# Attention with a conditioning token: another order of the score products in the last bursts of one core

## The chip, the cores and the metric

One NeuronCore of a Trainium2 chip runs the whole kernel; the other cores are idle. The metric is the device time of one execution in microseconds (us), as the median of several runs. All arithmetic but two small helpers is float32.

## The reference

`x` has shape (8, 512, 512): 8 batches, 512 rows, 512 features, which are 16 heads of 32. One token per batch, `cond_1024`, is projected and added to every row's query and key.

```python
Q = split_heads(x @ Wq.T + bq);  K = split_heads(x @ Wk.T + bk);  V = split_heads(x @ Wv.T + bv)
cQ = Q + split_heads(tokens @ Wq.T + bq)
cK = K + split_heads(tokens @ Wk.T + bk)
scores = einsum('bhqd,bhkd->bhqk', cQ, cK) / sqrt(32)
out = einsum('bhqk,bhkd->bhqd', softmax(scores, axis=-1), V)
return x + merge_heads(out)
```

## The kernel before

**Tiles.** The work is cut into T = 32 tiles `t`: 8 batches times 4 groups of 4 heads. The 4 heads of a tile lie in the 4 strips of 32 partitions, so a product over one head's 32 features uses one strip of 32 rows of TensorE's array, and the products of four heads can be in the array side by side. `qkT["q", t]` and `qkT["k", t]` hold a tile's transposed queries and keys.

**The softmax of one tile** goes in two passes over its scores. First the row maxima: `row_max(t, qc)` multiplies the queries of row block `qc` (128 rows, 4 blocks a tile) with all 512 keys, one product for each head (L499, in `row_scores`), each into a bank of PSUM, and VectorE (DVE) reduces the banks to negated maxima `nmax`: as two pairs of banks (L508, `row_max_of`), or for most tiles and the very last row block as two single banks (L490) and one pair. When the 4 blocks of a tile are done, `split_max` cuts the maxima into three bfloat16 parts (L532 to L535, on GpSimd (POOL), for the last tile on DVE), and `transpose_max` turns them with TensorE (L544) and copies them out as `maxT` (L550). Then the exponentials: `exponentials(t, kc)` computes the transposed scores of key block `kc`, for each head a product of `onesb` and `maxT` that writes the negated maxima into the bank (L560, bfloat16) and the score product added on top (L563), and ScalarE (ACT) takes the exponentials out of the four banks (L574, four instructions) into `e` tiles. `times_v(t, kc, ...)` multiplies them with V (L579); the 4 heads there use 4 strips of 32 columns.

A float32 product of 512 columns is two matmul instructions in the trace, a first and a second pass, each with its own weight load, so four heads show as x8.

**The order** is written out by hand. Each engine runs its instructions in program order (`tc.manual_schedule`), with the waits that the framework derives from tiles and PSUM banks. The main loop runs over t = 0 to 28. In a step a burst `exponentials(t, kc)`, `row_max(...)` is followed by projection products or by products with V. `TURNS` says which of the 8 banks a step uses: entries 0 to 3 are the banks of the four heads' scores in `exponentials`, entries 4 to 7 those of `row_max`; `banks(i, n)` reads the current row, and `row(i)` sets it to row 8 + i. The products after the burst use a bank of entries 0 to 3 whose exponentials are out.

**The last three tiles** (t = 29, 30, 31) have no projections left and stand below the loop. `part_of(t, bank, kcs)` multiplies some key blocks with V, ACT copies the bank out (L775, or L769 and an addition on POOL, L770); `masked` (L600, POOL), `spread_sums` (L610) and `denominators_of` (L780) make the denominators of tile 28 and 29, and `send_parts` divides (L785, L635 on DVE, L636 and L637 on POOL) and stores. For tiles 30 and 31 the denominators are sums of `e` tiles (`sum_of`, L845 and L847, mostly on DVE; L845 once on POOL) times a matrix of ones (`times_ones`, L589).

The bursts there, in order, with the tile and key block of the exponentials and the tile and row block of the maxima:

| burst | exponentials | maxima | after it |
|---|---|---|---|
| A | 29, 0 | 30, 1 | two products with V |
| B | 29, 1 | 30, 2 | one product with V |
| C | 29, 2 | 30, 3 | `split_max(30)` on POOL, one product with V, `spread_sums` |
| D | 29, 3 | 31, 0 | one product with V, `transpose_max(30)`, one more |
| E | 30, 0 | 31, 1 | two products with V, `spread_sums` |
| F | 30, 1 | 31, 2 | one product with V |
| G | 30, 2 | 31, 3 | `split_max(31)` on DVE, one product with V |
| H | 30, 3 | none | one product with V, then `transpose_max(31)` |
| I to L | 31, 0 to 3 | none | products with V and with ones |

Of the kernel before, what the change touches and what calls it, by code (L numbers as in the profile page):

```python
# [9 lines left out]
F32 = mybir.dt.float32  # L10
BF16 = mybir.dt.bfloat16
AF = mybir.ActivationFunctionType
ALU = mybir.AluOpType
AX = mybir.AxisListType
# [3 lines left out]
def kernel(  # L18
# [38 lines left out]
    nc = tc.nc  # L57
    P = 128
    B, S, D = x.shape
    HD = 32  # L60
    H = D // HD
    G = D // P
    HG = P // HD
# [12 lines left out]
    ep = ctx.enter_context(tc.tile_pool(name="ep", bufs=13))  # L76
# [15 lines left out]

# [4 lines left out]

# [11 lines left out]
    turn = [0]  # L109

    def banks(i, n=1):

        j = TURNS[turn[0]][i]
        if n == 1:
            return psum[:, j, :]
        k = TURNS[turn[0]][i + 1]
        return psum[:, j : k + 1 : k - j, :]
# [83 lines left out]
    onesb = const.tile([P, P], BF16, tag="onesb", name="onesb")  # L201
# [43 lines left out]
    for i in range(NS):  # L245
        r = slice(i * BL, (i + 1) * BL)
# [92 lines left out]
    qkT = {}  # L339
# [134 lines left out]
    nmax = {}  # L474
    sums = {}

    def open_max(t):
        if t not in nmax:
            nmax[t] = op.tile([P, NS, HG, 1], F32, tag="nmax", name=f"nmax_{t}", bufs=3)
            sums[t] = op.tile([P, NS, HG, 1], F32, tag="sums", name=f"sums_{t}", bufs=3)  # L480

    def row_max(t, qc):
        if t >= T:
            return
        open_max(t)
        for j in range(HG):
            row_scores(t, qc, j, banks(HG + j))
        if t < T - 2 or t * NS + qc == T * NS - 1:
            for j in range(2):
                nc.vector.tensor_reduce(  # L490
                    nmax[t][:, qc, j : j + 1, 0], banks(HG + j), AX.X, ALU.max, negate=True
                )
        else:
            row_max_of(t, qc, 0, banks(HG, 2))
        row_max_of(t, qc, 1, banks(HG + 2, 2))

    def row_scores(t, qc, j, pt):
        r = slice(j * HD, (j + 1) * HD)
        nc.tensor.matmul(  # L499
            pt,  # L500
            qkT["q", t][r, qc * P : (qc + 1) * P],
            qkT["k", t][r, :],
            start=True,
            stop=True,
        )

    def row_max_of(t, qc, pr, pt):
        nc.vector.tensor_reduce(  # L508
            nmax[t][:, qc, pr * 2 : pr * 2 + 2, 0], pt, AX.X, ALU.max, negate=True
        )  # L510
# [26 lines left out]
    maxT = {}  # L537

    def transpose_max(t, bank, copy=nc.vector.tensor_copy):
        if t >= T:  # L540
            return
        pt = bank.bitcast(BF16)
        for qc in range(NS):
            nc.tensor.transpose(  # L544
                pt[:, qc * P : (qc + 1) * P],
                split[t % 2][:, qc, :, :].rearrange("p h e -> p (h e)"),
                identb,
            )
        maxT[t] = op.tile([P, S], BF16, tag="maxT", name=f"maxT_{t}")
        copy(maxT[t], pt[:, :S])  # L550


    es = {}

    def exponentials(t, kc, at=None):

        bank = [psum[:, i, :] for i in at] if at else [banks(i) for i in range(HG)]
        for j in range(HG):
            r = slice(j * HD, j * HD + 3)
            nc.tensor.matmul(bank[j], onesb[r, :], maxT[t][r, :], start=True, stop=False)  # L560
        for j in range(HG):
            r = slice(j * HD, (j + 1) * HD)
            nc.tensor.matmul(  # L563
                bank[j],
                qkT["k", t][r, kc * P : (kc + 1) * P],
                qkT["q", t][r, :],
                start=False,
                stop=True,
            )
        for pr in range(NP):  # L570
            e = ep.tile([P, 2, S], F32, tag="e", name=f"e_{t}_{kc}_{pr}")
            es[t, kc, pr] = e
            for i in range(2):
                nc.scalar.activation(e[:, i, :], bank[pr * 2 + i], AF.Exp)  # L574

    def times_v(t, kc, pt, chunks=range(NS)):
        b, g = divmod(t, G)
        for j in range(HG):
            nc.tensor.matmul(  # L579
                pt[j * HD : (j + 1) * HD, :],  # L580
                vs[b % 2][:, kc, (g * HG + j) * HD : (g * HG + j + 1) * HD],
                es[t, kc, j // 2][:, j % 2, :],
                start=(kc == chunks[0]),
                stop=(kc == chunks[-1]),
            )
# [11 lines left out]
    def masked(t):  # L597

        apart = op.tile([P, HG, NS, NS], F32, tag="apart", name=f"apart_{t}")
        nc.gpsimd.tensor_tensor(  # L600
            apart,
            sums[t].rearrange("p c h o -> p h c o").broadcast_to([P, HG, NS, NS]),
            which.unsqueeze(1).unsqueeze(1).broadcast_to([P, HG, NS, NS]),
            ALU.mult,
        )
        return apart

    def spread_sums(apart, pd):
        for h in range(HG):
            nc.tensor.matmul(  # L610
                pd[h * BL : (h + 1) * BL, :NB],
                modulo,
                apart[:, h].rearrange("p c a -> p (c a)"),
                start=True,
                stop=True,
            )
# [63 lines left out]
    def bank(i):  # L680
        return psum[:, i, :]
# [48 lines left out]
        pass  # L730


    turn[0] = 12
    row_max(0, 0)
    turn_w("v", [1, 2, 3])
    combine_w("v")
# [24 lines left out]
    def part_of(t, pt, of, between=None):  # L761

        for k, kc in enumerate(of):
            if k and between:
                between()
            times_v(t, kc, pt, of)
        if t in parts:
            p = op.tile([P, S], F32, tag="dead", name=f"part_{t}_{of[0]}")
            nc.scalar.copy(p, pt)  # L769
            nc.gpsimd.tensor_tensor(parts[t], parts[t], p, ALU.add)  # L770
        else:
            if not parts:
                parts["all"] = stage.tile([P, NC, D], F32, tag="w", name="parts")
            parts[t] = parts["all"][:, t % NC, :]
            nc.scalar.copy(parts[t], pt)  # L775
# [12 lines left out]
    for t in range(T - 3):  # L788
        b, r = divmod(t, G)
# [52 lines left out]
    def sum_of(t, to, kc, on, prs=range(NP)):  # L842
        for pr in prs:
            if kc == 1:
                on.tensor_tensor(to[pr], es[t, 0, pr], es[t, 1, pr], ALU.add)  # L845
            else:
                on.tensor_tensor(to[pr], to[pr], es[t, kc, pr], ALU.add)  # L847
# [5 lines left out]
    def row(i):  # L853
        turn[0] = 8 + i

    t = T - 3
    row(0)
    exponentials(t, 0)
    row_max(t + 1, 1)
    part_of(t - 1, banks(0), [0, 1])  # L860
    load_residual(t + 1)
    load_residual(t + 2)
    row(1)
    exponentials(t, 1)
    row_max(t + 1, 2)
    part_of(t - 1, banks(0), [2])
    apart = masked(t - 1)
    row(2)
    exponentials(t, 2)
    row_max(t + 1, 3)  # L870
    split_max(t + 1)
    part_of(t - 1, banks(0), [3])
    spread_sums(apart, banks(1))
    den = denominators_of(t - 1, banks(1))
    row(3)
    exponentials(t, 3)
    row_max(t + 2, 0)
    part_of(t, banks(0), [0, 1], lambda: transpose_max(t + 1, banks(1), nc.scalar.copy))
    send_parts(t - 1, den)

    t = T - 2
    row(0)
    exponentials(t, 0)
    row_max(t + 1, 1)
    apart = masked(t - 1)
    part_of(t - 1, banks(0), [2, 3])
    spread_sums(apart, banks(1))
    den = denominators_of(t - 1, banks(1))
    row(1)
    exponentials(t, 1)  # L890
    row_max(t + 1, 2)
    acc = room_for_sums(t)
    sum_of(t, acc, 1, nc.gpsimd, [0])
    part_of(t, banks(0), [0])
    send_parts(t - 1, den)
    row(2)
    exponentials(t, 2)
    row_max(t + 1, 3)
    split_max(t + 1, nc.vector)
    pa, rest = banks(0), [1, 2, 3]  # L900
    times_v(t, 1, pa, rest)

    exponentials(t, 3, (1, 2, 3, 4))
    times_v(t, 2, pa, rest)
    transpose_max(t + 1, bank(5), nc.vector.tensor_copy)
    sum_of(t, acc, 1, nc.vector, [1])
    sum_of(t, acc, 2, nc.vector)

    t = T - 1
    exponentials(t, 0, (6, 7, 1, 2))  # L910
    times_v(t - 1, 3, pa, rest)
    nc.vector.tensor_tensor(parts[t - 1], pa, parts[t - 1], ALU.add)
    sum_of(t - 1, acc, 3, nc.vector)
    exponentials(t, 1, (3, 4, 5, 6))
    pv = bank(7)
    times_v(t, 0, pv)
    acc2 = room_for_sums(t)
    sum_of(t, acc2, 1, nc.vector)
    exponentials(t, 2, (1, 2, 3, 0))
    times_v(t, 1, pv)  # L920
    pd = bank(5)
    times_ones(acc, pd, True, True)
# [18 lines left out]
            queue.dma_start(spread(out[b], g * P + h * BL), y30[h * BL : (h + 1) * BL])  # L941

    store_30(nc.sync, (0, 1))
    exponentials(t, 3, (4, 6, 1, 2))
    times_v(t, 2, pv)
    pd = bank(3)
    times_ones(acc2, pd, True, False)
    times_ones([es[t, 3, pr] for pr in range(NP)], pd, False, True)
    times_v(t, 3, pv)
# [5 lines left out]
    nc.vector.tensor_copy(oT[:, two[0]], pv[:, two[0]])  # L955
    nc.scalar.copy(oT[:, two[1]], pv[:, two[1]])
    store_30(nc.scalar, (2, 3))
    pi, po = bank(0), [bank(4), bank(6)]
    untranspose(den, pi)
    rec = op.tile([P, NS, HG, 1], F32, tag="rec", name="rec")  # L960
    nc.vector.reciprocal(
# [52 lines left out]
```

## Time and profile before

| what | value |
|---|---|
| time, median of 3 runs | 731.7 us (731.52 to 732.57) |
| time of the profiled execution | 731.48 us |
| its span, first to last instruction | 729.7 us |
| mean granted TensorE clock | 0.999 |

The tail, by stretches of the span, busy us of each engine (PE is TensorE's matmuls, PEld its weight loads):

| stretch | PE | DVE | ACT | POOL |
|---|---|---|---|---|
| 680.5 to 706.5, bursts A to G | 26.00 | 17.35 | 18.42 | 12.24 |
| 706.5 to 723.5, bursts H to L | 16.20 | 16.25 | 10.98 | 2.17 |
| 723.5 to 729.7, last output | 1.44 | 2.16 | 0.37 | 1.44 |

How to read it: "busy" of PE runs from a matmul's start to a modelled end, so small idle times between bursts hardly show in it; they show as the bracket behind a row of the timeline, which gives the idle time just before it and what released it. In a row `PE L499 MATMUL psum<-kT,qT 32*128 32x512 f32 x8`, L499 is the line, `psum` what is written, `kT,qT` what is read, and x8 the number of instructions that follow each other.

### The profile page before, as it was taken

What the parts mean: (1) busy time and instruction counts of PE and PEld (TensorE: products, weight loads), DVE (VectorE), ACT (ScalarE), POOL (GpSimd) and SP (SyncE); (2) the same over time, 40 slices, a digit from 0 to 9 for tenths busy, and PEclk for the clock granted to TensorE, in tenths of its full rate; (3) what the DMA queues carried; (4) which work ended last, traced back from release to release, by engine and by line L of the source; (5) the groups of instructions that cost most, each with busy time, mean ns of one, the idle gap of its engine ahead of it and who ended that gap; (6) DMA issues with size and microseconds to landing.
All of it is one profiled execution on the core that took longest, in us unless ns stands there. A gap on an engine that the chain in (4) does not pass through costs nothing.

```text
span 729.7 us, 15089 instructions
## 1 busy us (share of the span) xinstructions
PE 722.4 (99%) x5396; PEld 402.0 (55%) x5396; DVE 536.9 (74%) x859; ACT 617.3 (85%) x1540; POOL 176.4 (24%) x276
## 2 busy tenths in 40 slices
PE   9999999999999999999999999999999999999997
PEld 5566555566555566555566555566555566555432
DVE  4798777777778777688676777677777777667677
ACT  2589898899898898898899898898898899898664
POOL 3711221122221122221122221122221122221351
PEclk9999999999999999999999999999999999999999
DMA  7733221222221222221222221222110111110121
GB/s 183 121 56 65 45 44 23 37 41 34 45 41 26 38 37 37 45 44 23 37 41 34 44 42 26 37 37 37 30 30 8 24 30 30 30 24 14 23 30 30
DMA packets 208111, 29.64 MB, mean 41 GB/s; under 512 B 205722, under 2 KB 206746, under 8 KB 208036
## 3 DMA queue, kind: packets, MB, share of 16 engines
q1 hardware_dynamic: 206400, 27.88, 23.9%
q10 hardware_dynamic: 1636, 0.81, 0.4%
q8 instruction: 42, 0.69, 0.4%
q14 instruction: 33, 0.27, 0.1%
HBM read 20.27 MB, written 8.39 MB: 39 GB/s over the span
## 4 chain that ended last, share of the span: by engine, by line
PE 97%; DVE 2%; issue 1%; DMA 1%; DVEq 0%
PE psum L406 26%; PE psum L499 16%; PE psum L579 15%; PE psum L563 15%; PE psum L403 14%; PE psum L560 6%; PE psum L350 2%; PE psum L544 1%; DVE acc L847 1%; DMA x<-in_x_dram 1%; PE psum L266 0%; DVE acc L845 0%; PE psum L311 0%; PE psum L657 0%; PE psum L589 0%
## 5 line engine op out<-in xcount | busy, mean ns | idle before, releaser
L518 ACT ACTIVATE dead<-psum,nmax 128x512 f32<-128x512 f32 x480 | 327.0, 701 | 5.4 <-DVE nmax L490 3.0
L574 ACT ACTIVATE e<-psum 128x512 f32<-128x512 f32 x512 | 264.3, 603 | 75.7 <-PE psum L563 75.6
L490 DVE TENSOR_REDUCE nmax<-psum 128x1 f32<-128x512 f32 x242 | 155.9, 686 | 143.2 <-PE psum L499 143.2
L508 DVE TENSOR_REDUCE nmax<-psum 128x2 f32<-128x1024 f32 x135 | 163.5, 1216 | 9.5 <-PE psum L499 8.2
L636 POOL TENSOR_TENSOR res<-res,recs 128x512 f32<-128x512 f32 x30 | 31.4, 1047 | 439.9 <-DVE res L635 439.9
L499 PE MATMUL psum<-kT,qT 32*128 32x512 f32 x1024 | 136.3, 601 | 0.0
L563 PE MATMUL psum<-qT,kT 32*128 32x512 f32 x1024 | 132.4, 588 | 0.0
L579 PE MATMUL psum<-e,v 128*32 128x512 f32 x1024 | 121.2, 596 | 0.0
L518 ACT ACTIVATION_READ_ACCUMULATOR dead<-psum,nmax 128x1 f32 x480 | 104.9, 218 | 0.0
L499 PEld LDWEIGHTS psum<-kT,qT 32*128 32x128 f32 x1024 | 58.1, 183 | 56.2 <-ACT dead L518 19.9
L579 PEld LDWEIGHTS psum<-e,v 128*32 128x32 f32 x1024 | 26.7, 110 | 65.8 <-issue 38.4
L563 PEld LDWEIGHTS psum<-qT,kT 32*128 32x128 f32 x1024 | 51.0, 185 | 2.2
L560 PE MATMUL psum<-maxT,onesb 3*128 3x512 bf16 x512 | 51.7, 384 | 0.5 <-DVE maxT L550 0.5
L403 PE MATMUL psum<-wc_v,xc 128*128 128x256 f32 x192 | 49.3, 379 | 0.0
L560 PEld LDWEIGHTS <-onesb 3*128 3x128 bf16 x512 | 13.4, 90 | 61.1 <-issue 51.7
L406 PE MATMUL psum<-xc,wc_k 128*128 128x256 f32 x180 | 46.2, 379 | 0.0
L406 PE MATMUL psum<-xc,wc_q 128*128 128x256 f32 x180 | 46.2, 379 | 0.0
L174 POOL TENSOR_TENSOR xr<-xr,bvs 128x512 f32<-128x512 f32 x31 | 39.3, 1268 | 17.8 <-DMA xr<-in_x_dram 17.8
L403 PEld LDWEIGHTS psum<-wc_v,xc 128*128 128x128 f32 x192 | 36.5, 190 | 5.0
L637 POOL TENSOR_TENSOR res<-res,xr 128x512 f32<-128x512 f32 x30 | 38.3, 1275 | 2.4
L403 PE MATMUL psum<-wT_v,xT 128*128 128x256 f32 x128 | 38.8, 405 | 0.0
L406 PEld LDWEIGHTS psum<-xc,wc_k 128*128 128x128 f32 x180 | 34.2, 190 | 4.6
(163 smaller groups left out, 775.2 us busy)
## 6 DMA issues: line engine op xcount, KB each, us to landing
xr<-in_x_dram SPq DMA_DIRECT2D x124, 64.0 KB, 2.4
out_dram<-res SPq DMA_DIRECT2D x122, 64.0 KB, 2.0
x<-in_x_dram SPq DMA_DIRECT2D x112, 64.0 KB, 2.5
w_q<-in_L_cond_Wq_dram SPq DMA_DIRECT2D x4, 256.0 KB, 4.5
w_v<-in_L_cond_Wv_dram SPq DMA_DIRECT2D x16, 64.0 KB, 2.4
w_k<-in_L_cond_Wk_dram SPq DMA_DIRECT2D x16, 48.0 KB, 2.2
x<-in_x_dram ACTq DMA_DIRECT2D x2, 256.0 KB, 4.3
x<-in_x_dram SPq DMA_DIRECT2D x2, 256.0 KB
```

Source lines behind the costliest of these rows:

```text
L174: nc.gpsimd.tensor_tensor(xr[t], xr[t], bias, ALU.add)
L403: nc.tensor.matmul(pt, xb, w, start=(kc == kcs[0]), stop=(kc == kcs[-1]))
L406: nc.tensor.matmul(pt, w, xb, start=(kc == kcs[0]), stop=(kc == kcs[-1]))
L490: nc.vector.tensor_reduce(nmax[t][:, qc, j : j + 1, 0], banks(HG + j), AX.X, ALU.max, negate=True)
L499: nc.tensor.matmul(pt, qkT["q", t][r, qc * P : (qc + 1) * P], qkT["k", t][r, :], start=True, stop=True,)
L508: nc.vector.tensor_reduce(nmax[t][:, qc, pr * 2 : pr * 2 + 2, 0], pt, AX.X, ALU.max, negate=True)
L518: nc.scalar.activation(dead, banks(HG + j), AF.Exp, bias=nmax[t][:, qc, j, :], accum_out=sums[t][:, qc, j, :],)
L560: nc.tensor.matmul(bank[j], onesb[r, :], maxT[t][r, :], start=True, stop=False)
L563: nc.tensor.matmul(bank[j], qkT["k", t][r, kc * P : (kc + 1) * P], qkT["q", t][r, :], start=False, stop=True,)
L574: nc.scalar.activation(e[:, i, :], bank[pr * 2 + i], AF.Exp)
L579: nc.tensor.matmul(pt[j * HD : (j + 1) * HD, :], vs[b % 2][:, kc, (g * HG + j) * HD : (g * HG + j + 1) * HD], es[t, kc, j // 2][:, j % 2, ...
L637: nc.gpsimd.tensor_tensor(y, y, xr.pop(t), ALU.add)
```

## The change

Bursts B to G call a new function `crossed` in place of `exponentials` and `row_max`. In it heads 0 and 1 have their maxima products ahead of their scores, and heads 2 and 3 have them behind; the exponentials of heads 2 and 3 are taken first; and the maxima are always reduced as two single banks and a pair. Burst A keeps its order (`row(4)` has the banks that `row(0)` had). The rows of `TURNS` for these bursts are other ones: the maxima always use banks 0 to 3, the scores banks 4 to 7 in changing order; the products with V go to the bank of head 2. The sum on POOL takes the pair of heads 2 and 3, DVE's the other. In H `transpose_max(31)` stands ahead of the product with V. The banks of H to L and of the last output are other ones. The line ahead of the loop that sets `turn[0] = 12` sets 13, since a row of `TURNS` was added ahead of that one; the loop's own rows are the same.

```diff
+        (6, 7, 4, 5, 0, 1, 2, 3),
+        (7, 4, 5, 6, 0, 1, 2, 3),
         (4, 5, 6, 7, 0, 1, 2, 3),
-        (6, 7, 0, 1, 2, 3, 4, 5),
-        (0, 1, 2, 3, 4, 5, 6, 7),
-        (2, 3, 4, 5, 6, 7, 0, 1),
+        (5, 6, 7, 4, 0, 1, 2, 3),
+        (4, 5, 6, 7, 0, 1, 2, 3),
...
+    def crossed(t, kc, qc, u=None):
+        u = u or t + 1
+        open_max(u)
+        bank = [banks(i) for i in range(HG)]
+        def maxima(js):
+            for j in js:
+                row_scores(u, qc, j, banks(HG + j))
+        def scores(js):
+            for j in js:
+                r = slice(j * HD, j * HD + 3)
+                nc.tensor.matmul(bank[j], onesb[r, :], maxT[t][r, :], start=True, stop=False)
+            for j in js:
+                r = slice(j * HD, (j + 1) * HD)
+                nc.tensor.matmul(bank[j], qkT["k", t][r, kc * P : (kc + 1) * P],
+                    qkT["q", t][r, :], start=False, stop=True)
+        maxima((0, 1))
+        scores((2, 3))
+        scores((0, 1))
+        maxima((2, 3))
+        for pr in (1, 0):
+            e = ep.tile([P, 2, S], F32, tag="e", name=f"e_{t}_{kc}_{pr}")
+            es[t, kc, pr] = e
+            for i in range(2):
+                nc.scalar.activation(e[:, i, :], bank[pr * 2 + i], AF.Exp)
+        for j in range(2):
+            nc.vector.tensor_reduce(
+                nmax[u][:, qc, j : j + 1, 0], banks(HG + j), AX.X, ALU.max, negate=True)
+        row_max_of(u, qc, 1, banks(HG + 2, 2))
     t = T - 3
-    row(0)
+    row(4)
     exponentials(t, 0)
     row_max(t + 1, 1)
     part_of(t - 1, banks(0), [0, 1])
...
     row(1)
-    exponentials(t, 1)
-    row_max(t + 1, 2)
-    part_of(t - 1, banks(0), [2])
+    crossed(t, 1, 2)
+    part_of(t - 1, banks(2), [2])
...
     row(3)
-    exponentials(t, 3)
-    row_max(t + 2, 0)
-    part_of(t, banks(0), [0, 1], lambda: transpose_max(t + 1, banks(1), nc.scalar.copy))
+    crossed(t, 3, 0, t + 2)
+    part_of(t, banks(2), [0, 1], lambda: transpose_max(t + 1, banks(3), nc.scalar.copy))
...
-    sum_of(t, acc, 1, nc.gpsimd, [0])
-    part_of(t, banks(0), [0])
+    sum_of(t, acc, 1, nc.gpsimd, [1])
+    part_of(t, banks(2), [0])
...
-    pa, rest = banks(0), [1, 2, 3]
+    pa, rest = banks(2), [1, 2, 3]
     times_v(t, 1, pa, rest)
-    exponentials(t, 3, (1, 2, 3, 4))
+    exponentials(t, 3, (0, 1, 7, 4))
+    transpose_max(t + 1, bank(5), nc.vector.tensor_copy)
     times_v(t, 2, pa, rest)
-    transpose_max(t + 1, bank(5), nc.vector.tensor_copy)
-    sum_of(t, acc, 1, nc.vector, [1])
+    sum_of(t, acc, 1, nc.vector, [0])
     sum_of(t, acc, 2, nc.vector)
...
```

More of the change, by code (lines that the diff above doesn't have):

```diff
@@ L730, in nothing @@
         pass
-    turn[0] = 12
+    turn[0] = 13
     row_max(0, 0)
@@ L854, in row @@
         turn[0] = 8 + i
+    def crossed(t, kc, qc, u=None):
[11 more added lines that the diff above has]
+                r = slice(j * HD, (j + 1) * HD)
+                nc.tensor.matmul(
+                    bank[j],
+                    qkT["k", t][r, kc * P : (kc + 1) * P],
+                    qkT["q", t][r, :],
+                    start=False,
+                    stop=True,
+                )
+        maxima((0, 1))
[9 more added lines that the diff above has]
+            nc.vector.tensor_reduce(
+                nmax[u][:, qc, j : j + 1, 0], banks(HG + j), AX.X, ALU.max, negate=True
+            )
+        row_max_of(u, qc, 1, banks(HG + 2, 2))
     t = T - 3
-    row(0)
+    row(4)
     exponentials(t, 0)
@@ L863 @@
     row(1)
-    exponentials(t, 1)
-    row_max(t + 1, 2)
-    part_of(t - 1, banks(0), [2])
+    crossed(t, 1, 2)
+    part_of(t - 1, banks(2), [2])
     apart = masked(t - 1)
     row(2)
-    exponentials(t, 2)
-    row_max(t + 1, 3)
+    crossed(t, 2, 3)
     split_max(t + 1)
-    part_of(t - 1, banks(0), [3])
+    part_of(t - 1, banks(2), [3])
     spread_sums(apart, banks(1))
@@ L882 @@
     row(0)
-    exponentials(t, 0)
-    row_max(t + 1, 1)
+    crossed(t, 0, 1)
     apart = masked(t - 1)
-    part_of(t - 1, banks(0), [2, 3])
+    part_of(t - 1, banks(2), [2, 3])
     spread_sums(apart, banks(1))
@@ L889 @@
     row(1)
-    exponentials(t, 1)
-    row_max(t + 1, 2)
+    crossed(t, 1, 2)
     acc = room_for_sums(t)
-    sum_of(t, acc, 1, nc.gpsimd, [0])
-    part_of(t, banks(0), [0])
+    sum_of(t, acc, 1, nc.gpsimd, [1])
+    part_of(t, banks(2), [0])
     send_parts(t - 1, den)
     row(2)
-    exponentials(t, 2)
-    row_max(t + 1, 3)
+    crossed(t, 2, 3)
     split_max(t + 1, nc.vector)
-    pa, rest = banks(0), [1, 2, 3]
+    pa, rest = banks(2), [1, 2, 3]
     times_v(t, 1, pa, rest)
-    exponentials(t, 3, (1, 2, 3, 4))
+    exponentials(t, 3, (0, 1, 7, 4))
+    transpose_max(t + 1, bank(5), nc.vector.tensor_copy)
     times_v(t, 2, pa, rest)
-    transpose_max(t + 1, bank(5), nc.vector.tensor_copy)
-    sum_of(t, acc, 1, nc.vector, [1])
+    sum_of(t, acc, 1, nc.vector, [0])
     sum_of(t, acc, 2, nc.vector)
     t = T - 1
-    exponentials(t, 0, (6, 7, 1, 2))
+    exponentials(t, 0, (2, 3, 0, 1))
     times_v(t - 1, 3, pa, rest)
@@ L913 @@
     sum_of(t - 1, acc, 3, nc.vector)
-    exponentials(t, 1, (3, 4, 5, 6))
-    pv = bank(7)
+    exponentials(t, 1, (7, 4, 5, 2))
+    pv = bank(3)
     times_v(t, 0, pv)
@@ L918 @@
     sum_of(t, acc2, 1, nc.vector)
-    exponentials(t, 2, (1, 2, 3, 0))
+    exponentials(t, 2, (0, 1, 7, 6))
     times_v(t, 1, pv)
@@ L943 @@
     store_30(nc.sync, (0, 1))
-    exponentials(t, 3, (4, 6, 1, 2))
+    exponentials(t, 3, (4, 2, 0, 1))
     times_v(t, 2, pv)
-    pd = bank(3)
+    pd = bank(7)
     times_ones(acc2, pd, True, False)
@@ L957 @@
     store_30(nc.scalar, (2, 3))
-    pi, po = bank(0), [bank(4), bank(6)]
+    pi, po = bank(6), [bank(4), bank(2)]
     untranspose(den, pi)
```

## The prediction

> **What bounds the kernel now.** I read the page first, then the chain of waits in order of time for the last 25 us, then the timeline there. On the page TensorE is never idle:
>
> ```profile
> PE 722.4 (99%) x5396; PEld 402.0 (55%) x5396; DVE 536.9 (74%) x859; ACT 617.3 (85%) x1540; POOL 176.4 (24%) x276
> PE 97%; DVE 2%; issue 1%; DMA 1%; DVEq 0%
> ```
>
> The change lies in the last 50 us, and there the chain tells more than the shares. It leaves TensorE after burst G's maxima products and stays on DVE to the last sum:
>
> ```profile
> 704.59 1.06 PE psum L499 x8
> 705.65 1.27 DVE nmax L490 x2
> 706.92 1.14 DVE nmax L508
> ...
> 709.07 0.41 PE psum L544 x4
> ...
> 709.85 1.22 DVE acc L845
> ...
> 713.86 2.35 DVE acc L847 x2
> 716.21 1.19 DVE acc L845 x2
> ...
> 719.53 1.23 DVE acc L847
> 720.76 0.04 issue
> ```
>
> So the end is set by the time at which burst G's last reduction is done (708.06). From there split (0.96), turn, copy and 10.9 us of sums (709.85 to 720.75) follow with no gap on DVE that another engine could fill. Ahead of that, the bursts follow each other on TensorE, some with stalls:
>
> ```profile
> 684.41 0.10 PEld L560 LDWEIGHTS <-onesb 3*128 3x128 bf16 x4 [0.84 <-issue]
> 685.50 1.03 PE L499 MATMUL psum<-kT,qT 32*128 32x512 f32 x8
> 686.45 0.16 PEld L579 LDWEIGHTS psum<-e,v 128*32 128x32 f32 x8 [0.76 <-ACT e L574]
> 687.45 0.09 PEld L560 LDWEIGHTS <-onesb 3*128 3x128 bf16 x2 [0.84 <-issue]
> 687.81 0.13 PEld L560 LDWEIGHTS <-onesb 3*128 3x128 bf16 x2 [0.27 <-issue]
> 688.98 1.14 PE L499 MATMUL psum<-kT,qT 32*128 32x512 f32 x8
> ```
>
> Burst B from 684.41 to 687.45 is the undisturbed unit, 3.04 us: 0.23 for the broadcasts (L560), 0.86 for scores, 0.86 for maxima, 0.09 to the product with V, 1.00 for that. In burst C the second pair of broadcasts comes 0.36 late (687.81), since its banks are only then reduced and read, and its maxima's weights were not loaded ahead (1.14 instead of 1.03, so 0.11). C takes 3.64. D and G have the same stall (691.09 and 702.94).
>
> **The change, part by part.**
>
> *Work on TensorE.* No product is added. One strip does maxima (0.86), broadcast (0.22), score (0.86), the other broadcast, score, maxima: 1.94 each, as before. Two things must hold. First, products of different strips must pass each other: heads 2 and 3 have to run their broadcasts and scores while the second passes of heads 0 and 1's maxima still wait. The trace has a case, in columns instead of rows, near the end, where the program has all four products of `acc` ahead of those of `e`:
>
> ```profile
> 720.81 0.62 PE L589 MATMUL psum<-e,ones 128*32 128x512 f32 x2
> 720.83 0.12 PEld L589 LDWEIGHTS psum<-acc,ones 128*32 128x32 f32 x2
> 721.25 0.60 PE L589 MATMUL psum<-acc,ones 128*32 128x512 f32 x2
> ```
>
> The first passes of `e` start 0.44 ahead of the second passes of `acc`, which precede them in the program. The Trainium skill ("TensorE: Matmul & The Clock Gate", Part 3, "The mechanism") says the contrary: matmuls keep program order at start and end, and only weight loads are pulled ahead. By that rule the sum would be the first rival's, 733.4 us; I go by the row. Second, the burst now begins with a float32 product whose weights are not there: 0.11 more by the C row, where a broadcast begins at once. So a unit becomes about 3.1, and six bursts lose at most 0.66 together; the bound below is nothing.
>
> *Stalls removed.* Heads 2 and 3's scores are out at the same point of the burst as before, so the exponentials start there, and heads 0 and 1's follow with no gap (ACT 2.06 a burst, plus 0.58 or 0.76 of copies, under 3.1). The maxima of heads 0 and 1 are out a whole product earlier, so DVE starts about 1 us sooner. With single reductions it takes 2.43 (705.63 to 708.06) where pairs took 2.36. All waits of C, D and G are then met before they are needed: burst C's third broadcast, say, needs bank 6, whose exponential is B's second. The closest are ACT's copies, which heads 0 and 1's broadcasts need: 0.09 to 0.2 us to spare in B, C, F and G. That cover gone, a late copy is paid in full.
>
> *A wait added.* `spread_sums` in C and E writes the bank of head 1, whose exponential is now the last. In C it is done at about 690.85 (scores of heads 0 and 1 end 689.53, 0.20 to ACT, 0.48 for head 0, 0.62 for head 1), and the product with V ends at 690.50: TensorE waits about 0.4, with burst D behind it. In E two products with V cover it.
>
> *Walk of the burst starts* (before, then after): B 684.41, 684.41; C 687.45, 687.50; D 691.09, 691.10 (the wait just named eats C's gain); E 695.95, 695.52 (D's stall gone: 0.33 and 0.11); F 699.90, 699.54; G 702.94, 702.62; product with V after G 705.54, 704.74 (G's stall gone).
>
> *Burst G's maxima.* The product with V of F ends at 702.53; 0.2 later the first maxima stream, they end 703.59, and DVE can read 0.2 later. DVE itself is free from the reciprocal and turn of tile 29 (0.81, L785 and L635, after F's reductions end at about 703.1) at 703.86. So the three reductions run from 703.86 instead of 705.63: 706.29 instead of 708.06. That is -1.77.
>
> *The turned maxima ahead of a product.* Split ends 707.25. TensorE is done with H's scores at 706.8 and waits for it. Left behind the product with V (0.95), the turn would come at 707.9, so the move is worth about 0.5 on DVE, and the idle time on TensorE costs nothing while DVE sets the end. DVE's sums are the same instructions, nine of 1.2 us and one of 0.68; the pair swapped to POOL (2.35) is done by 704.3, long before DVE needs it.
>
> *Other banks and queues.* SP's loads and stores keep their places. POOL gets the same instructions, each ready earlier. No DMA is moved past another. The banks of H to L I cost at nothing: each waits for exponentials two bursts back.
>
> *Is DVE still last?* With everything 1.77 sooner the last sum ends at 718.98 and frees TensorE at 719.03. ACT's last exponentials, walked by TensorE's order and 2.06 a burst, end at 719.4; TensorE needs them 0.88 after it is freed, at 719.9. So 0.5 is to spare: DVE sets the end, and a gain over 2.3 would be cut there.
>
> **Sum.** 731.48 - 1.77 = 729.7 for the profiled execution. The median shown is 0.2 above that one, so 729.9. The own range of this case: 729.3 if the burst's first load costs nothing and C's wait is shorter (0.6 less), 730.6 if each of the six bursts takes 0.11 more than I reckoned (0.66 more).
>
> **Rivals.**
>
> *Strict order of passes: slower.* If a second pass that waits holds up all that the program has behind it, a burst runs so, with 0.43 a pass: maxima of heads 0 and 1 at 0 and 0.43; the other strips' broadcasts only at 0.43, their scores at 0.64 and 1.07; broadcasts of heads 0 and 1 at 1.07, their scores at 1.28 and 1.71; maxima of heads 2 and 3 at 1.71 and 2.13, done at 2.56. That is 2.56 instead of 1.92, six times. The walk then reaches the product after G at 708.5 and the last reduction (1.2 after the last maxima) at 709.8, 1.7 later than now: 733.4 us. It decides from the first burst in which a strip's product can't pass a waiting second pass. Against it stands the row at 720.81.
>
> *A wait takes the stalls' place.* If ACT's copies come 0.3 later than walked, four bursts lose up to 0.2 each, on top of C: the gain falls to 1.0, 730.7 us. For it: margins of 0.09 to 0.2; against it: ACT has 0.3 a burst idle.
>
> *The last stage doesn't pass it on.* If TensorE and ACT, which gain 0.80 at G, become the bound below, the end moves by 0.80: 730.9 us. For it: only 0.5 to spare; against it: ACT is idle before each of H, I and L now (1.25, 1.37, 1.05).
>
> **How the numbers follow.** Forecast 0.62, strict order 0.15, waits in place 0.15, last stage 0.08. What this measurement can tell from no change is about 0.2%, 1.46 us: under 730.2 is faster, over 733.2 slower. The forecast's own range lies two thirds or more below 730.2, with a part of it and most of the two middle cases within 0.2%; the strict order lies just over it. So faster 0.56, same 0.28, slower 0.16. The range must take in the forecast and the middle cases, and can leave out the strict order: 729.2 to 731.6.
>
> **What would show it.** Right: in B to G the broadcasts of heads 2 and 3 start within 0.1 of the first maxima; no idle time from DVE or ACT ahead of a broadcast; one wait of about 0.4 ahead of the sums' spread in C; product after G at about 704.7; last reduction done at about 706.3; DVE's sums without a gap to about 719.0. Wrong: first score passes of heads 2 and 3 over 1 us after the first maxima, or ACT's last exponentials later than the last sum.

## The result, and the profile after

| | before | after |
|---|---|---|
| median of 22 runs each | 731.53 us (731.36 to 732.57) | 730.47 us (730.14 to 731.74) |
| ratio, 95% interval | | 0.9985 (0.9979 to 0.9991) |
| profiled execution | 731.48 us, span 729.7 | 730.29 us, span 728.5 |

The change saves 1.06 us; 1.77 were forecast. The median lies inside the range, but I had given 0.56 to a time under 730.2 us and 0.28 to one from there to 733.2, and it is the second that came.

Most line numbers have moved down by one: L500 is the maxima products, L545 the turn, L551 its copy, L580 the products with V, L846 and L848 the sums. `crossed` holds L871 (broadcasts), L874 (scores), L890 (exponentials) and L892 (single reductions).

The page's engine line and the chain's shares say nothing new:

```profile
PE 721.3 (99%) x5396; PEld 402.7 (55%) x5396; DVE 537.3 (74%) x864; ACT 617.3 (85%) x1540; POOL 176.3 (24%) x276
PE 96%; DVE 2%; issue 1%; DMA 0%; ACT 0%; DVEq 0%
```

Burst B in the timeline of TensorE (start, duration, what) shows the new order running as drawn. The broadcasts (L871) start 0.02 after the first maxima, and the scores of heads 2 and 3 run ahead of the second passes of the maxima (684.88), which the program has in front of them. Lower down the first passes of the maxima of heads 2 and 3 (685.45) start ahead of the scores of heads 0 and 1 (685.52), which stand before them in the program too:

```profile
684.34 0.70 PE L500 MATMUL psum<-kT,qT 32*128 32x512 f32 x2
684.36 0.39 PE L871 MATMUL psum<-maxT,onesb 3*128 3x512 bf16 x2
684.58 0.59 PE L874 MATMUL psum<-qT,kT 32*128 32x512 f32 x2
684.88 0.59 PE L500 MATMUL psum<-kT,qT 32*128 32x512 f32 x2
...
685.45 0.59 PE L500 MATMUL psum<-kT,qT 32*128 32x512 f32 x2
685.52 0.59 PE L874 MATMUL psum<-qT,kT 32*128 32x512 f32 x2
...
686.48 1.07 PE L580 MATMUL psum<-e,v 128*32 128x512 f32 x8
687.47 0.70 PE L500 MATMUL psum<-kT,qT 32*128 32x512 f32 x2
```

The end of burst C has the wait that was reckoned, ahead of the sums' spread, and D starts behind it:

```profile
690.98 0.26 PE L611 MATMUL psum<-apart,modulo 128*32 128x16 f32 x8 [0.31 <-ACT e L890]
691.17 0.70 PE L500 MATMUL psum<-kT,qT 32*128 32x512 f32 x2
```

The chain of waits from burst G on (start, duration, piece) leaves TensorE 1.68 earlier than before (703.97 for 705.65) but the copy (L551) starts only 1.34 earlier (708.17 for 709.51):

```profile
703.97 1.27 DVE nmax L892 x2
705.24 1.14 DVE nmax L509
706.40 0.49 DVE split L533
...
707.66 0.41 PE psum L545 x4
...
708.17 0.42 DVE maxT L551
708.59 1.14 DVE acc L846
709.76 1.64 DVE acc L848 x2
...
718.31 1.23 DVE acc L848
```

The copy in the timeline of DVE of the kernel before:

```profile
709.51 0.42 DVE L550 COPY maxT<-psum 128x512 bf16<-128x512 bf16 x1 [0.49 <-PE psum L544]
```

**A yardstick.** Medians of one kernel in different groups of runs differ by up to 0.3 us, and the last addition of a projection, ahead of the bursts, starts between 680.65 and 681.12 in most of the profiled executions. For small sizes I use a stretch inside the trace: from the start of that addition on DVE (680.71 before, 680.65 after) to the end of its last sum. It falls into four parts, with the same instructions in every kernel but for the edit shown. The last column is the median less the median of the kernel before in the same group of runs.

| kernel | to G's first reduction | G's reductions | from there to the copy's start | copy to last sum's end | whole stretch | median, against before |
|---|---|---|---|---|---|---|
| before | 24.92 | 2.42 | 1.46 | 11.24 | 40.03 | |
| after | 23.31 | 2.42 | 1.80 | 11.36 | 38.88 | -1.06 |
| e1 plain order | 32.02 | 2.42 | 1.52 | 11.36 | 47.32 | +7.08 |
| e2 turn behind | 23.30 | 2.42 | 2.24 | 11.36 | 39.33 | -0.87 |
| e3 sums' bank | 22.91 | 2.42 | 1.81 | 11.36 | 38.50 | -1.43 |
| e4 broadcasts first | 23.33 | 2.42 | 1.79 | 11.36 | 38.90 | -1.26 |
| e5 no addition | 23.30 | 2.42 | 1.52 | 11.36 | 38.60 | -1.42 |
| e6 G plain | 24.94 | 2.42 | 1.52 | 11.36 | 40.24 | +0.21 |
| e7 reduction as cast | 23.30 | 2.42 | 1.56 | 11.36 | 38.65 | -1.33 |
| e8 before, turn ahead | 24.92 | 2.42 | 1.45 | 11.24 | 40.03 | +0.09 |
| e9 order of sums | 23.31 | 2.42 | 1.80 | 11.24 | 38.76 | -1.19 |
| e10 three edits | 22.91 | 2.42 | 1.57 | 11.24 | 38.14 | -1.86 |
| e11 e10, a sum on POOL | 22.91 | 2.42 | 1.57 | 12.28 | 39.18 | -0.75 |
| e12 a sum on POOL | 23.31 | 2.42 | 1.80 | 12.40 | 39.93 | +0.17 |

So the change moved the stretch by -1.61, +0.34 and +0.12, in all -1.15, and the medians by -1.06. Behind the last sum 8.9 to 9.0 us pass in every kernel. The profiled executions of e3 and e12 lost 3 and 2 us far ahead of the bursts, which the stretch leaves out.

### The profile page after: what moved, and what is told of

Its sections match the earlier page's. It is cut to its first block, busy times and chain, and to the rows that moved or that the text cites. A ratio compares the mean times of both kernels' runs of the same rounds, so it can differ in the third digit from the quotient of the medians.

```text
span 728.5 us, 15084 instructions
## 1 busy us (share of the span) xinstructions
PE 721.3 (99%) x5396; PEld 402.7 (55%) x5396; DVE 537.3 (74%) x864; ACT 617.3 (85%) x1540; POOL 176.3 (24%) x276
## 4 chain that ended last, share of the span: by engine, by line
PE 96%; DVE 2%; issue 1%; DMA 0%; ACT 0%; DVEq 0%
PE psum L407 26%; PE psum L500 16%; PE psum L580 15%; PE psum L404 14%; PE psum L564 14%; PE psum L561 5%; PE psum L351 2%; PE psum L545 1%; DVE acc L848 1%; PE psum L874 1%; DMA x<-in_x_dram 0%; PE psum L267 0%; DVE acc L846 0%; PE psum L312 0%; ACT e L890 0%
## 5 line engine op out<-in xcount | busy, mean ns | idle before, releaser
L575 ACT ACTIVATE e<-psum 128x512 f32<-128x512 f32 x488 | 251.9, 603 | 71.3 <-PE psum L564 71.0
L509 DVE TENSOR_REDUCE nmax<-psum 128x2 f32<-128x1024 f32 x130 | 157.6, 1214 | 2.7 <-PE psum L500 2.7
L500 PE MATMUL psum<-kT,qT 32*128 32x512 f32 x1024 | 142.5, 601 | 0.0
L564 PE MATMUL psum<-qT,kT 32*128 32x512 f32 x976 | 125.5, 587 | 0.0
L580 PE MATMUL psum<-e,v 128*32 128x512 f32 x1024 | 121.2, 596 | 0.0
L500 PEld LDWEIGHTS psum<-kT,qT 32*128 32x128 f32 x1024 | 59.7, 183 | 57.1 <-ACT dead L519 19.9
L580 PEld LDWEIGHTS psum<-e,v 128*32 128x32 f32 x1024 | 26.6, 110 | 65.1 <-issue 37.6
L564 PEld LDWEIGHTS psum<-qT,kT 32*128 32x128 f32 x976 | 48.6, 185 | 2.2
L561 PE MATMUL psum<-maxT,onesb 3*128 3x512 bf16 x488 | 48.1, 385 | 0.0
L407 PEld LDWEIGHTS psum<-xc,wc_q 128*128 128x128 f32 x180 | 34.2, 190 | 4.7
```

Source lines behind the costliest of these rows:

```text
L407: nc.tensor.matmul(pt, w, xb, start=(kc == kcs[0]), stop=(kc == kcs[-1]))
L500: nc.tensor.matmul(pt, qkT["q", t][r, qc * P : (qc + 1) * P], qkT["k", t][r, :], start=True, stop=True,)
L509: nc.vector.tensor_reduce(nmax[t][:, qc, pr * 2 : pr * 2 + 2, 0], pt, AX.X, ALU.max, negate=True)
L564: nc.tensor.matmul(bank[j], qkT["k", t][r, kc * P : (kc + 1) * P], qkT["q", t][r, :], start=False, stop=True,)
L580: nc.tensor.matmul(pt[j * HD : (j + 1) * HD, :], vs[b % 2][:, kc, (g * HG + j) * HD : (g * HG + j + 1) * HD], es[t, kc, j // 2][:, j % 2, ...
```

## The experiments

Every kernel here is the kernel after with the edit shown, except e8, which is the kernel before with one edit.

**Does the order bring the gain, or the banks?** e1 puts the old order into `crossed`:

```diff
-        maxima((0, 1))
-        scores((2, 3))
-        scores((0, 1))
-        maxima((2, 3))
-        for pr in (1, 0):
+        scores((0, 1, 2, 3))
+        maxima((0, 1, 2, 3))
+        for pr in (0, 1):
```

> The changed kernel, with the six bursts back in plain order (all broadcasts, all scores, then all maxima; exponentials of heads 0 and 1 first), but on the new banks and with the turn still ahead of the product. Theory 'the order brings it': each stalled burst takes some 0.36 longer and burst G's first maxima come a whole product (0.86 to 1.06 us) later, so DVE's reductions of G start at about 705.6 instead of 703.95 and the end comes 1.0 to 1.7 us later, 731.5 to 732.2 us. Rival 'the banks bring it': the stalls went because of the other banks; then the bursts keep their length and only G's own reductions are late, at most 0.9: 731.2 us or less, with no stall in C, D or G.

It took 738.87 us, and both theories missed it. The timeline of TensorE around burst C shows what I had overlooked:

```profile
688.00 1.06 PE L580 MATMUL psum<-e,v 128*32 128x512 f32 x8 [0.68 <-ACT e L888]
689.00 0.38 PE L871 MATMUL psum<-maxT,onesb 3*128 3x512 bf16 x1
689.83 0.39 PE L871 MATMUL psum<-maxT,onesb 3*128 3x512 bf16 x3 [0.44 <-ACT part L770]
```

The product with V goes to head 2's bank, which in the old order is read third and not first; so V waits 0.68 for ACT, and the next broadcast, behind the copy of that bank, 0.44 more. Each burst from B to G has such waits (0.68 or 0.78 at V, 0.39 to 0.79 at a broadcast). The new banks without the new order are worse than either kernel; e1 does not tell how the gain divides.

**Which burst brings it?** e6 leaves B to F crossed and puts G alone in plain order, with banks that suit that order (6, 7, 4, 5 for heads 0 to 3, V on the first of them):

```diff
-    row(2)
-    crossed(t, 2, 3)
+    row(0)
+    crossed(t, 2, 3, plain=True)
...
-    pa, rest = banks(2), [1, 2, 3]
+    pa, rest = banks(0), [1, 2, 3]
```

> The changed kernel with burst G alone in plain order (broadcasts, scores, maxima; exponentials of heads 0 and 1 first; its banks 6, 7, 4, 5 for heads 0 to 3, so that the earliest read come first, the product with V on head 0's). Theory 'G's own order brings most': bank 5 holds F's part until ACT has copied it (703.5), so G's scores start at about 703.55 and its first maxima come at about 704.4; DVE's reductions start at 705.3 instead of 703.95, and the end comes 1.35 later, 731.8 us. Rival 'the walk of the bursts ahead brings most' (0.44 of it at D, kept to G): G's own order is worth 0.5 at most, 731.0 us or less.

It took 731.89 us, as the theory had it, which is the time of the kernel before (ratio 0.9999, 0.9990 to 1.0008), and 1.36 more on the stretch than after. The timeline of TensorE in G: the broadcasts wait for banks, and the first maxima come only at 705.01.

```profile
703.27 1.14 PE L871 MATMUL psum<-maxT,onesb 3*128 3x512 bf16 x4
704.05 1.23 PE L874 MATMUL psum<-qT,kT 32*128 32x512 f32 x8
705.01 1.12 PE L500 MATMUL psum<-kT,qT 32*128 32x512 f32 x8
```

G's reductions start 24.94 into the stretch, with before's 24.92 beside it. Without G's own order nothing of the gain is left; the five crossed bursts ahead of it bring G's start from 22.23 (702.94 - 680.71) to 22.14 (702.79 - 680.65) and no further. That G alone in the new order would do as well was not run.

**What would C's wait be worth?** e3 spreads the sums into head 3's bank, whose exponential is read second, and from D on lets banks 4, 5 and 7 trade places:

```diff
+        (7, 6, 4, 5, 0, 1, 2, 3),
+        (6, 4, 5, 7, 0, 1, 2, 3),
+        (4, 5, 7, 6, 0, 1, 2, 3),
+        (5, 7, 6, 4, 0, 1, 2, 3),
...
-    spread_sums(apart, banks(1))
-    den = denominators_of(t - 1, banks(1))
-    row(3)
+    spread_sums(apart, banks(3))
+    den = denominators_of(t - 1, banks(3))
+    row(14)
...
```

> The changed kernel with the sums' spread in burst C on the bank of head 3, whose exponential is read second, in place of head 1's, which is read last; from burst D on the banks 4, 5 and 7 trade places (4 to 5, 5 to 7, 7 to 4), so that D again first takes banks that are free. Theory: the wait of 0.31 ahead of the spread (690.98) goes, D starts about 0.3 earlier (690.85), and since every later burst follows TensorE, G and the last sum come 0.3 earlier too: 730.2 us. Rival: D's reductions wait for POOL's split (692.34) and not for TensorE, and the gain is lost by burst E: 730.5 us.

The wait is gone: D starts 0.16 behind the spread's start, and that 0.88 behind the product with V.

```profile
692.69 1.06 PE L584 MATMUL psum<-e,v 128*32 128x512 f32 x8
693.57 0.23 PE L615 MATMUL psum<-apart,modulo 128*32 128x16 f32 x8
693.73 0.70 PE L504 MATMUL psum<-kT,qT 32*128 32x512 f32 x2
```

D starts 0.51 earlier on the stretch (693.73 - 683.72 = 10.01, for 691.17 - 680.65 = 10.52). G's reductions come 0.40 earlier, and the median follows (-1.43 against -1.06 of after). The rest goes in D itself: its first two broadcasts take 0.59 together, 0.39 elsewhere, since the second one has the bank that C's last exponential leaves at 693.91. The rival's wait is not there: DVE's reductions in D start at 694.96, before POOL's split is done (695.43).

**Does the burst's first load cost 0.11?** e4 puts the broadcasts of heads 2 and 3 ahead of the maxima of heads 0 and 1 (`broadcasts` is the first half of `scores`):

```diff
+        broadcasts((2, 3))
         maxima((0, 1))
         scores((2, 3))
+        broadcasts((0, 1))
         scores((0, 1))
         maxima((2, 3))
```

> The changed kernel with the broadcasts of heads 2 and 3 ahead of the maxima of heads 0 and 1 in each of the six bursts. Theory: the burst's first float32 load (0.11 a burst, the row of 0.70 where the others have 0.59) is then hidden behind the broadcasts, which take the array's other rows, so a burst takes 0.05 to 0.11 less; G starts 0.25 to 0.5 earlier, the end moves by about as much: 730.0 to 730.2 us. Rival: the maxima are held up by the broadcasts ahead of them (0.2 a burst, since a later instruction passes an earlier one only where that one waits), G's reductions start 0.1 to 0.2 later: 730.6 us or more.

Nothing moved (38.90 for 38.88 us on the stretch), and the row of 0.70 stands in each burst as before: the broadcasts do not hide the load of the first product's weights, which starts with that product, and do not delay the maxima either. Both theories fall, and the load stays in the open at either place.

**Is the turn ahead of the product worth 0.5?** e2 puts it back behind; e8 puts it ahead in the kernel before.

```diff
-    transpose_max(t + 1, bank(5), nc.vector.tensor_copy)
     times_v(t, 2, pa, rest)
+    transpose_max(t + 1, bank(5), nc.vector.tensor_copy)
```

> The changed kernel with the turned maxima put back behind burst H's product with V (nothing else changed). By my sum the move was worth 0.5 us on DVE: split ends 707.61, the product with V holds TensorE until 707.95 or so, so the copy on DVE starts 0.3 to 0.5 later and the end comes as much later, 730.8 to 731.0 us. Rival: the product with V, which has nothing to wait for, runs out in the time in which TensorE waits for split anyway, and the move is worth under 0.1: 730.5 us.

> The kernel before with only the turn of the last maxima put ahead of H's product with V. There split ends at 709.02 and the product with V is over by then, so DVE gains nothing, and TensorE does the product 0.95 later, into a slack that I put at 0.5 to 1: 731.5 to 731.9 us. Rival: the turn ahead of the product is worth something without the crossed bursts too: 731.2 us or less.

e2 takes 730.92 us, and the time to the copy grows from 1.80 to 2.24: the 0.44 is there. e8 takes 731.77 us, with the stretch at 40.03 as before. Both as expected: the turn's place is worth 0.44 only where split comes before TensorE has finished that product, and split does so through G's earlier maxima.

**Why is split 0.27 longer?** Its first cast took 0.48 (0.21 before), beside POOL's addition of tile 29's residual. e5 leaves that addition out, e7 keeps it and writes the cast as a reduction over one element. The edit of e5, then of e7:

```diff
-        nc.gpsimd.tensor_tensor(y, y, xr.pop(t), ALU.add)
+        x = xr.pop(t)
+        if t != T - 3:
+            nc.gpsimd.tensor_tensor(y, y, x, ALU.add)
```

```diff
-        on.tensor_copy(sp[:, :, :, 0:1], m)
+        if on is nc.vector:
+            on.tensor_reduce(sp[:, :, :, 0], m, AX.X, ALU.max)
+        else:
+            on.tensor_copy(sp[:, :, :, 0:1], m)
```

> The changed kernel without POOL's addition of the residual to tile 29 (1.27 us, 705.56 to 706.83; this addition is left out, all else is there). Theory 'POOL holds the cast up': split's first cast on DVE (0.48 at 706.40, where it took 0.21 before) ended 0.05 after that addition; without it the cast takes 0.2, split ends 0.27 earlier and the last sum as much: 730.2 us. Rival: the cast is long for another reason (what DVE did ahead of it) and stays at 0.48: 730.5 us.

> The changed kernel with the first cast of burst G's split written as a reduction over one element (same values, DVE, no cast). If only the cast is held up by POOL's addition: 0.2 to 0.25 instead of 0.48, split ends 0.2 to 0.27 earlier, 730.2 to 730.3 us. Rival: the subtraction behind it, which reads two tiles of SBUF, is then held up in its place until POOL ends at 706.83: gain 0.1 at most, 730.4 us.

The timelines of POOL and DVE, first of the kernel after, where the cast ends 0.05 behind the addition (705.56 + 1.27 = 706.83):

```profile
705.56 1.27 POOL L638 TENSOR_TENSOR res<-res,xr 128x512 f32<-128x512 f32 x1
706.40 0.48 DVE L533 CAST split<-nmax 128x16 bf16<-128x16 f32 x1
```

then of the kernel before, where the addition is over when the cast comes (706.35 + 1.27 = 707.62):

```profile
706.35 1.27 POOL L637 TENSOR_TENSOR res<-res,xr 128x512 f32<-128x512 f32 x1
708.09 0.21 DVE L532 CAST split<-nmax 128x16 bf16<-128x16 f32 x1
```

then of e5, without the addition:

```profile
706.62 0.20 DVE L533 CAST split<-nmax 128x16 bf16<-128x16 f32 x1
```

and of e7, with the addition under way and a reduction in the cast's place:

```profile
705.89 1.27 POOL L641 TENSOR_TENSOR res<-res,xr 128x512 f32<-128x512 f32 x1
706.74 0.22 DVE L534 TENSOR_REDUCE split<-nmax 128x16 bf16<-128x16 f32 x1
706.99 0.21 DVE L537 TENSOR_TENSOR rest<-nmax,split 128x16 f32<-128x16 f32 x1
```

The cast waits for POOL, the reduction does not, and the stretch shrinks by 0.28 and 0.23. The Trainium skill has this in "SBUF — State Buffer", section "Who interferes with whom": VectorE and GpSimd share a pair of ports, a cast can take both of VectorE's and then has to wait until GpSimd lets go, a reduction never does. The rows agree on both counts. The subtraction behind e7's reduction reads two tiles of SBUF; it took 0.21 for 0.18 and ended 0.04 behind the addition (707.20, 707.16), so it may have been held for a moment, as the rival had it, at a price of some 0.03. The change brought the cast 1.69 forward and POOL's addition only 0.79 (706.35 to 705.56).

**Why are the sums 0.12 longer?** The pair given to POOL was swapped, so DVE's first sum writes pair 0 and the next one reads it. e9 turns the second round around:

```diff
-    sum_of(t, acc, 2, nc.vector)
+    sum_of(t, acc, 2, nc.vector, [1, 0])
```

> The changed kernel with DVE's second round of sums of tile 30 in the order pair 1, pair 0, so that the first of them does not read what the instruction just ahead of it wrote. Theory 'the swap of the pair given to POOL put two dependent sums next to each other': the sum behind the first starts 1.13 after it, as before, in place of 1.25, and from the copy to the last sum it takes 11.24 in place of 11.36 us: 0.12 less, 730.35 us. Rival: the 0.12 is the wait for another engine and stays.

The timeline of DVE, of the kernel after and of e9; the second sum starts 1.25 and 1.13 behind the first:

```profile
708.51 1.22 DVE L846 TENSOR_TENSOR acc<-e,e 128x1024 f32<-128x1024 f32 x1
709.76 1.23 DVE L848 TENSOR_TENSOR acc<-acc,e 128x1024 f32<-128x1024 f32 x1
```

```profile
708.58 1.22 DVE L846 TENSOR_TENSOR acc<-e,e 128x1024 f32<-128x1024 f32 x1
709.71 2.35 DVE L848 TENSOR_TENSOR acc<-acc,e 128x1024 f32<-128x1024 f32 x2
```

The 0.12 is back on the stretch (11.24), as the theory said; the median (730.29 us) can't resolve it alone.

**A better version, and what bounds it.** e10 has the edits of e3, e7 and e9. e11 and e12 give one more sum (tile 31, pair 0) to POOL, on top of e10 and on top of after.

```diff
-    sum_of(t, acc2, 1, nc.vector)
+    sum_of(t, acc2, 1, nc.gpsimd, [0])
+    sum_of(t, acc2, 1, nc.vector, [1])
```

> The changed kernel with three edits together: the sums' spread in C on head 3's bank, the first cast as a reduction, the sums in the order pair 1, pair 0. If the three terms add up (0.38, 0.23 and 0.12 in their own traces): 0.73 less from the last product ahead of the bursts to the last sum, 38.15 in place of 38.88 us, 729.7 us. Rival: with DVE 0.7 earlier, ACT's last exponentials (0.28 behind the last sum now) set the end, and the time behind the last sum grows by as much as is saved beyond 0.3: 730.1 us.

> The kernel of the three edits, and besides one of tile 31's first sums (pair 0, 1.2 us on DVE) on POOL, which is idle from 706.83 to 721. Theory: POOL needs 2.36 for it beside DVE and is done before DVE wants it; DVE's last sum comes 1.15 earlier and TensorE and ACT set the end, with 0.3 to 0.9 gained: 728.8 to 729.4 us. Rival: POOL and DVE, both reading two tiles of SBUF, hold each other up, DVE's sums beside POOL's take 2 us in place of 1.2, and nothing is gained: 729.7 us or more.

> The changed kernel with only that sum of tile 31 on POOL. If DVE alone sets the end and the next bound is TensorE and ACT with the 0.5 that I reckoned or up to 0.9: 729.6 to 730.0 us. Rival: the two engines hold each other up, or ACT's last exponentials set the end at once: 730.4 us.

e10 takes 729.62 us, ratio to before 0.9972 (0.9961 to 0.9983), the best of all kernels run. Its stretch is 38.14, and the three terms from their own traces give 38.88 - 0.38 - 0.23 - 0.12 = 38.15. Its chain of waits stays on TensorE from the turn on:

```profile
707.23 0.40 PE psum L552 x4
707.63 1.00 PE psum L587 x8
...
718.23 2.28 PE psum L597 x14
```

That view counts TensorE as busy up to modelled ends. The timeline shows that the product with the last sum still waits for DVE: its weights are loaded 0.06 behind the end of that sum (716.62 + 2.35 = 718.97).

```profile
716.62 2.35 DVE L855 TENSOR_TENSOR acc<-acc,e 128x1024 f32<-128x1024 f32 x2
719.03 0.11 PEld L597 LDWEIGHTS psum<-acc,ones 128*32 128x32 f32 x2 [0.86 <-DVE acc L855]
```

The passes ahead of that product start at 718.47, and passes of this size follow each other 0.43 apart here, so TensorE could have started it at 718.90. By this estimate DVE is last by only 0.13. What brings the turn forward, as the edits of e3 and e7 do, moves both engines; what shortens the sums alone has 0.13 left to gain in e10, and by the same reckoning 0.24 in the kernel after (718.91 + 0.43 = 719.34, for 719.58).

e11 and e12 are 1.1 and 1.2 us slower than e10 and after (730.73 and 731.65 us), and 1.04 and 1.05 on the stretch. In e11, POOL's sum stands first, and DVE's sum beside it takes 3.40, where it takes 1.2 alone:

```profile
713.02 3.47 POOL L853 TENSOR_TENSOR acc<-e,e 128x1024 f32<-128x1024 f32 x1 [6.55 <-ACT e L582]
714.18 3.40 DVE L853 TENSOR_TENSOR acc<-e,e 128x1024 f32<-128x1024 f32 x1
```

The rivals held in kind, but had 2 us for DVE's sum and no loss. DVE's sum ends at 717.58, 1.09 behind POOL's end (716.49), about the time of a sum; and POOL's own 3.47, for 2.36 in F, began while DVE was still at its sums (to 714.26). So in these rows additions that read two tiles of SBUF run one after the other, and either engine can be the one that waits. By the estimate above there was little to gain in any case: 0.13 in e11, where the theory had 0.3 to 0.9. POOL's sum in F cost DVE nothing: the reductions beside it read PSUM and took 1.21 as always.

## Why the prediction was right, and which terms were off

- **Passes overtake: right.** Broadcasts of heads 2 and 3 come 0.02 behind the first maxima in B; the strict order would have had them at 0.43 or later. The rule of the Trainium skill ("TensorE: Matmul & The Clock Gate", Part 3, "The mechanism") that matmuls start and end in program order does not hold in these rows, where the products lie in different strips. Program order is here the order of the kernel's text; a trace does not show how the compiled passes stand.
- **The unit: slightly short.** B to C and F to G take 3.13 (687.47 - 684.34, 702.79 - 699.66), 3.08 to 3.09 in the walk. C, D and E also cost up to 0.1 more than walked, so B to G takes 18.45 for 18.21. The 0.70 of the first load is as reckoned.
- **Stalls and the added wait: right in kind.** No broadcast waits for a bank, no late copy of ACT holds one up; C's wait is there (0.31 ahead of the sums' spread); by e3 it costs 0.51 at D's start and 0.40 at G's reductions.
- **G's maxima: right, and the source of the gain.** G's first reduction came 1.61 earlier on the stretch, for 1.77 in the sum; the rest is the 0.24 of the walk less 0.08 which DVE needed less to get from G's start to its reduction. e6 puts a number to what I had left implicit: without G's own order nothing is left.
- **The turn ahead: right.** I put it at about 0.5; e2 measured 0.44.
- **Split, turn and copy: the term that was off most.** I let the time from the last reduction to the copy stand as before, and it grew by 0.34. Of that 0.27 or so is the cast that waits for POOL (e5, e7). The other 0.07 is between turn and copy: 0.51 from one to the other, 0.44 before. In the kernel after the copy waits for TensorE and for ACT, before for TensorE alone; that this second wait costs the 0.07 was not tried. It is not the turn's place: with the new banks and the turn behind (e2) it is 0.51 (708.46 to 708.97), with the old banks and the turn ahead (e8) 0.44 (709.27 to 709.71).
- **DVE's sums: the second one.** "The same instructions" was true, but not in the same neighbourhood: 0.12 for the dependence (e9).
- **What bounds next: one term missed.** I let a gain over 2.3 be cut, by the 0.5 that ACT's last exponentials had to spare. e10's gain, 1.89 on the stretch, does not reach that; all of it comes through to the end, and ACT still has 0.53 (ended 719.38, needed 719.91). What I did not reckon is that TensorE's own passes come within 0.13 of DVE there.
- **The signs.** Those of being right came, with the product after G at 704.93 for 704.7 and the last sum at 719.53 for 719.0. One of being wrong came too: ACT's last exponentials end at 719.82, 0.29 behind the last sum. It was badly chosen, since my own walk had them 0.4 behind (719.4 for 718.98), and TensorE needs them only at 720.46.

The sum by the measured terms: 1.61 - 0.34 - 0.12 = 1.15 saved, 1.06 between the medians. The range, 729.2 to 731.6, would also have held two of the rivals (730.7 and 730.9), so the time alone decides little; the rows do. Of the rivals, strict order did not happen; ACT's copies were in time, so that 730.5 lies near that rival's 730.7 is chance; and the last stage passed on all that it was given (8.94 and 8.95 behind the last sum).

## What to carry to other kernels

When one engine's chain is pulled forward by a microsecond or two, check what the others are doing at the new time: a short cast that was free of POOL may now run into it, and a reduction in its place does not. Banks and order belong together, since whoever is read first must own the bank that is reused first. When one engine is last, also see by how much: the next one may be 0.1 us behind. And before swapping equal pieces of work between engines, see which neighbours then depend on each other.

## What the runs showed of the hardware that I had not expected

- A bfloat16 cast of 16 elements on DVE took 0.48 in place of 0.20 while POOL added two float32 tiles; a one-element reduction with the same result took 0.22 there.
- DVE and POOL additions with two operands in SBUF held each other up: in e11 3.40 in place of 1.2 on DVE, 3.47 in place of 2.36 on POOL.
- A DVE addition that reads what the one ahead of it wrote started 0.12 later (1.25 for 1.13).
- Broadcasts put ahead of a strip's float32 product did not shorten it (0.70 where the later ones have 0.59), though they run in other rows.
- Float32 products on different strips of rows did not start in the order of the program: 685.45 for a later one, 685.52 for an earlier one.
